# Transposes of linear attention: VectorE blocks of 32 x 32 and transfers through scratch in place of TensorE products

## The chip, the cores and the metric

The kernel runs on one core of a Trainium2 chip. The time is device microseconds (us) of one execution. The kernel before took 2965.23, 2965.16 and 2964.53 us in three runs; the median is 2965.16. The profile is of one further execution.

## The reference

Four residual layers, each with a GroupNorm ahead of it, work on four images of 256 channels and 64 x 64 pixels. The change touches the second layer, and the kernel overlaps it with the first layer of the next image.

```python
x = x + conv_and_nonlocal(gn(x))      # 3x3 convolution, then attention over 4096 x 4096 pixels
x = x + linear_attention(gn(x))       # the layer that is changed
x = x + generated_convolution(gn(x))  # 3x3 depthwise and pointwise, filters made from the image
x = x + mixture_of_experts(gn(x))     # 1x1 convolution

def linear_attention(x):              # x: b, 256, 64, 64
    xn = rmsnorm(x, g_norm)           # over the 256 channels of a pixel
    q, k, v = split(einsum('oc,bchw->bohw', w_qkv, xn))       # 4 heads of 32 each
    q = softmax(q, over the 32 channels of a head)
    k = softmax(k, over the pixels)
    context = einsum('bhdn,bhen->bhde', k, v)
    out = einsum('bhde,bhdn->bhen', context, q * 32 ** -0.5)
    out = einsum('oc,bchw->bohw', w_out, out) + b_out
    return rmsnorm(out, g_out)
```

## The kernel before

**Rounds.** Everything is float32. In round b the generator `attend(b)` (L1068) computes the nonlocal attention of image b in 128 steps: 8 blocks of 512 queries, 16 steps each, a step being 256 keys. A step issues two products of logits (`pf`, L1101), two exponentials on ScalarE (`pr`, L1102), and the products with the values of the step before (`py`). For most blocks these are two wide products (L1217), and VectorE keeps a running sum `tot` of the exponentials (L137); for some blocks of the later images they are eight "turned" products of 129 columns (L1214), which bring the sum with them and need no VectorE. There are 512 steps in the four rounds.

**The chain beside it.** While image b attends, the rest of image b-1 is worked off: `tail(b-1)` is `nonlocal_out`, `linear_attention` (L1352), `generated` and `mixed`, and after it comes the convolution of image b+1. `Chain` (L50) sets these between the steps: each `yield n` of the tail adds n times a rate to a credit, and each whole credit lets one attention step be issued. The rate is 0.775 in rounds 1 and 2 and 1.14 in round 3, where only tail(2) is beside the attention. `yield None` is exactly one step. Tail(3) has no attention beside it (`alone`); its code is another branch. The order of instructions on each engine is the order in which the program issues them (a manual schedule); a wait in one holds back all behind it on its engine. So where a `yield` stands, and what is issued before it, sets what stands beside what. `w.fill` and `w.settle` issue pieces that are held back and play a part in tails 2 and 3 only.

**Linear attention of a chunk of 512 pixels** (8 chunks to an image). `normed` (L1369) applies the GroupNorm, one half of the channels on ScalarE, the other on VectorE, with the channels on the partitions. `turned` (L1379) brings the pixels onto the partitions: eight TensorE transposes, products of 128 x 128 with an identity (L1387), into two PSUM banks; ScalarE squares and sums each pixel's 256 channels (L1389); VectorE clamps, and GpSimd takes the power -1/2 (`rsqrt`, L230 to L232). `tokens` (L1395) multiplies by that root into `xt` on VectorE. `product` and `qk_of` (L1404, L1411) make q and k of the pixels by eight products, exponentials on ScalarE with the root as scale, and the softmax over q on VectorE. `context` (L1427) transposes q with four more products (L1431), which ScalarE copies to `qT` (L1432), and adds k times `xt` to the bank `pctx` in four products of 257 columns, of which the last is a column of ones: the sum of k.

```python
for c in range(NC):
    if c + 1 < NC:
        ahead = normed(c + 1)
...
    yield 0.5
    this = (yield from qk_of(xg, rinv, first)), xt
    first = ()
    if c + 1 < NC:
        xg = ahead
        rinv, banks = turned(xg)
    if last is not None:
        context(c - 1, *last)
```

Four small products then fold the context with the weights of v and of the output into `w2`. In the second loop (L1579) `outputs` (L1509) makes 512 pixels of the output by four products with `w2`, pixels on the partitions, and ScalarE squares them; `root` is as before; `scaled` (L1525) writes `z`, half of it by one VectorE operation, half by two on ScalarE; `added` (L1540) brings the channels back to the partitions by eight transposes (L1545), adds to the image `big` and takes its statistics (`bn_stats`, L1547). The next GroupNorm waits for these: `group_finish` (L396) aggregates them on VectorE and multiplies by a block average on TensorE (`pm`, L413).

**Memory.** `ra` and `rt` are buffers of the convolution and are free during linear attention; the outermost columns of `ra` must be zero when the convolution begins. The pool `k4` has nine buffers of 512 x 4 floats a partition, `k2` four of 512, and PSUM eight banks. `copy_x` (L777) starts DMAs that copy image b+2 into scratch. DMAs are issued by SP (SyncE), one after another, most of them for all parts of the program.

Of the kernel before, what the change touches and what calls it, by code (L numbers as in the profile page):

```python
# [13 lines left out]
P = 128  # L14
NH = 2
# [22 lines left out]
IX1 = HW // MX1  # L38
RW = MX * (IX + 1)
TURNED = 2  # L40
US_A_STEP = 4.35
EASED = 0.68

# [60 lines left out]
def conv_preact_fast(ctx: ExitStack, tc: tile.TileContext, guard, in_range, x, wc, wtpg, ww, wqkv, wout, w1cat, wd2,  # L104
# [153 lines left out]

    rows_d = tc.dram_tile([TY, P, NH, 3, NH * P], F32, name="rows_d")
    filters = tc.dram_tile([TY, P, TX - 2, NH, NH * P], F32, name="filters")  # L260
    taps = wc_s.rearrange("p h (i j) o -> p h i (j o)", i=3)

    NU = TY * NH * 3 * NH * P
# [1088 lines left out]
    def linear_attention(w, b, big, qT, k4, st, sh, sums):  # L1352
# [16 lines left out]
        def normed(c):  # L1369
            cols = bass.ts(c, 512)  # L1370
            xg = k4("xg").rearrange("p (h n) -> p h n", h=NH)
            for h in range(NH):
                if h == 1 and (c == 0 or not alone):
                    nc.vector.tensor_scalar(xg[:, h, :], big[:, h, cols], rstd[:, h:h + 1], nb[:, h:h + 1], ALU.mult, ALU.add)
                else:
                    nc.scalar.activation(xg[:, h, :], big[:, h, cols], AF.Identity, bias=nb[:, h:h + 1], scale=rstd[:, h:h + 1])
            return xg

        def turned(xg):  # L1379

            rinv = sp.tile([P, 4], F32, name="rinv", bufs=4)
            banks = []
            for s in range(2):
                ps = bank("ps_xt").rearrange("p (j c) -> p j c", j=2)
                for j in range(2):
                    for h in range(NH):
                        nc.tensor.transpose(ps[:, j, bass.ts(h, P)], xg[:, h, bass.ts(2 * s + j, P)], ident)  # L1387
                for j in range(2):
                    nc.scalar.activation(junk()[:, 0:NH * P], ps[:, j, :], AF.Square, accum_out=rinv[:, 2 * s + j:2 * s + j + 1])  # L1389
                banks.append(ps)  # L1390
            nc.vector.tensor_scalar(rinv, rinv, 1e-24, None, ALU.max)
            rsqrt(rinv, rinv)
            return rinv, banks

        def tokens(rinv, banks):  # L1395

            xt = k4_wide("xt").rearrange("p (j c) -> p j c", j=4)
            nc.gpsimd.memset(xt[:, :, NH * P:NH * P + 1], 1.0)
            for s in range(2):
# [26 lines left out]

        def context(c, qk, xt):  # L1427

            pt = bank("ps_qt")
            for j in range(4):  # L1430
                nc.tensor.transpose(pt[:, bass.ts(j, P)], qk[:, j, 0:HID], ident)  # L1431
            nc.scalar.copy(qT[:, bass.ts(c, 512)], pt)  # L1432
            for j in range(4):
                nc.tensor.matmul(pctx[:, 0:NH * P + 1], qk[:, j, HID:2 * HID], xt[:, j, :],
                                 start=(c == 0 and j == 0), stop=(c == NC - 1 and j == 3))

        if alone:
            w.fill(1)
            warm(3)
        w.settle()  # L1440
        xg, first = normed(0), ()
        if not alone:
            yield None
        rinv, banks = turned(xg)
        if alone:
            first = [product(xg, j) for j in range(2)]
            next(sums)
        xt = tokens(rinv, banks)
        yield 1
        last = None  # L1450
        for c in range(NC):
            if c + 1 < NC:
                ahead = normed(c + 1)
            if alone:
                next(sums, None)
                if c == 2:
                    checks.append(counted())
                if c in (2, 4, 5):
                    next(checks[0])
            elif b + 2 < B and c % 2 == 0:  # L1460
                copy_x(b + 2, c // 2)
            yield 0.5
            this = (yield from qk_of(xg, rinv, first)), xt
            first = ()
            if c + 1 < NC:
                xg = ahead
                rinv, banks = turned(xg)
            if last is not None:
                context(c - 1, *last)
            if c + 1 < NC:  # L1470
                xt = tokens(rinv, banks)
            last = this
        yield 1
        context(NC - 1, *last)
        w.fill(1)
        rk = sp.tile([P, 1], F32, name="rk", bufs=1)
        nc.vector.reciprocal(rk, pctx[:, NH * P:NH * P + 1])
        cx = k2("cx")[:, 0:NH * P]
        nc.vector.tensor_scalar(cx, pctx[:, 0:NH * P], rk, None, ALU.mult)
        yield None  # L1480
        pt = bank("ps_cx")
        for h in range(NH):
# [17 lines left out]
        if alone:  # L1500
            warm(2)
        w2 = k2("w2")[:, 0:NH * P]
        stt(w2, pw[:, 0:NH * P], HD * float(HD) ** -0.5, bo_s, ALU.mult, ALU.add)
        w.settle()
        yield None

# [18 lines left out]
        def scaled(zr, banks):  # L1525
            z = k4("z").rearrange("p (j o) -> p j o", j=4)
            if alone:
                for j in range(4):
                    src = banks[j // 2][:, j % 2, :]
                    if j < 3:  # L1530
                        nc.scalar.activation(z[:, j, :], src, AF.Copy, scale=zr[:, j:j + 1])
                    else:
                        nc.vector.tensor_scalar(z[:, j, :], src, zr[:, j:j + 1], None, ALU.mult)
                return z
            tt(z[:, 0:2, :], banks[0], zr[:, 0:2].unsqueeze(2).to_broadcast([P, 2, NH * P]), ALU.mult)
            for j in (2, 3):
                nc.scalar.activation(z[:, j, :], banks[1][:, j - 2, :], AF.Copy, scale=zr[:, j:j + 1])
            return z

        def added(c, z, halves=range(NH)):  # L1540
# [34 lines left out]
            w.fill(3)  # L1575
            return st, early, centre

        last = None
        for c in range(NC):  # L1579
            zb = outputs(c)  # L1580
            root(zb[0])
            yield 0.65
            if last is not None:
                added(c - 1, last)
            last = scaled(*zb)
            w.settle()
            if c in (2, 4):
                w.fill(1)
            yield 0.65
        yield 1  # L1590
        added(NC - 1, last)
        return st


# [558 lines left out]
    with tc.manual_schedule(engines={E.PE, E.Activation, E.DVE, E.Pool, E.SP}):  # L2153
        run(Chain(convolve_first).steps())
        run(project(first=True))
        for b in range(B - 1):
            attention = attend(b)
            parts = [tail(b - 1, big, qT), lambda w: convolve(w, b + 1, 0.53)] if b > 0 else [
                scale_weights, filters_across, lambda w: convolve(w, 1, 0.87)]
            if b == 0:  # L2160
                load_x(1)
            run(Chain(both(*parts), 1.365 if b == 0 else 0.775).steps(), attention)
# [594 lines left out]
```

## Time and profile before

The profiled execution took 2965.21 us; the span from its first to its last instruction is 2963.3 us. The granted clock of TensorE was 0.999 over the span.

| what | busy, mean of one | count |
|---|---|---|
| logits products L1101 | 966.4 us, 594 ns | 2048 |
| exponentials L1102 (ScalarE) | 602.8 us, 596 ns | 1024 |
| running sums L137 (VectorE, 1024 columns) | 307.7 us, 1221 ns | 252 |
| transposes of the output L1545 | 29.6 us, 274 ns | 224 records |
| transposes of the queries L1431 | 15.0 us, 273 ns | 100 records |
| copies of the queries L1432 (ScalarE, rounds) | 13.9 us, 580 ns | 24 |
| squares L1389 (ScalarE, 256 columns from PSUM) | 49.2 us, 384 ns, and 195 ns to read the sum | 128 |
| context products L1434, first form | 47.6 us, 380 ns | 200 records |

Each row is a group of instructions of one line and one shape. The duration of a product runs from its start to its modelled end, and products overlap; their spacing is read from the starts in the timeline. A few of TensorE's records are missing from the trace, so the counts of products can be a little low. In the prediction's lines, "idle before, releaser" at the end of a row is the time for which the engine stood still just ahead of the group, and what ended it; in a timeline the first number is the start and the second the length of a run of like instructions.

### The profile page before, as it was taken

How to read it: one execution, taken by the hardware profiler on the slowest of the kernel's cores; microseconds unless marked ns; L12 is line 12 of the kernel's file. 1: busy time of each engine (PE TensorE's matmuls, PEld its weight loads, DVE VectorE, ACT ScalarE, POOL GpSimd, SP SyncE). 2: the span in 40 equal slices, each digit the busy share in tenths (PEclk: the TensorE clock that was granted, in tenths of full speed). 3: DMA queues.
4: the chain of work that ended last, by engine and by line, in shares of the span. 5: the costliest groups of instructions: out<-in, count | busy, mean ns of one | idle time of the engine just before them, and what ended most of it. 6: DMA issues, size and time to landing. Idle time of an engine off the chain costs nothing. (4 is left out here: it accounts for less than half of the span.)

```text
span 2963.3 us, 31330 instructions
## 1 busy us (share of the span) xinstructions
PE 2917.0 (98%) x11638; PEld 1777.7 (60%) x11638; DVE 1786.2 (60%) x2792; ACT 1353.8 (46%) x2720; POOL 189.4 (6%) x235
## 2 busy tenths in 40 slices
PE   7999999999999999999999999999999999999999
PEld 3454555556566666777566666677646544446744
DVE  8737767751545863775355584477344568873585
ACT  2234333345656444225565543333555454433774
POOL 0000000001001000000001000000000100000143
PEclk9999999999999999999999999999999999999999
DMA  6245444324322021111640302211342223225111
GB/s 228 73 88 121 69 62 75 47 32 100 114 40 35 30 79 70 55 57 28 147 93 4 54 12 97 79 50 50 82 107 18 17 28 63 25 32 142 43 67 77
DMA packets 371297, 199.38 MB, mean 67 GB/s; under 512 B 305665, under 2 KB 315649, under 8 KB 367617
## 3 DMA queue, kind: packets, MB, share of 16 engines
q1 hardware_dynamic: 71328, 175.81, 17.5%
q10 hardware_dynamic: 295200, 4.72, 8.0%
q0 software_dynamic: 4608, 16.78, 3.7%
q8 instruction: 93, 1.52, 0.2%
q14 instruction: 68, 0.55, 0.1%
HBM read 131.18 MB, written 82.87 MB: 72 GB/s over the span
## 5 line engine op out<-in xcount | busy, mean ns | idle before, releaser
L1102 ACT ACTIVATE pr<-pf 128x512 f32<-128x512 f32 x1024 | 602.8, 596 | 911.4 <-PE pf L1101 888.7
L1101 PE MATMUL pf<-tpg 128*128 128x512 f32 x2048 | 966.4, 594 | 0.0
L1101 PEld LDWEIGHTS pf<-tpg 128*128 128x128 f32 x2048 | 374.1, 190 | 358.4 <-issue 336.6
L1217 PE MATMUL py<-pr,tpg 128*128 128x512 f32 x1152 | 541.6, 592 | 0.9 <-ACT pr L1102 0.9
L1214 PEld LDWEIGHTS py<-tpg,pr 128*128 128x128 f32 x3584 | 434.9, 192 | 108.0 <-issue 100.7
L1214 PE MATMUL py<-tpg,pr 128*128 128x129 f32 x3584 | 436.3, 275 | 2.4 <-ACT pr L1102 2.4
L1217 PEld LDWEIGHTS py<-pr,tpg 128*128 128x128 f32 x1152 | 218.6, 190 | 277.5 <-issue 268.6
L137 DVE TENSOR_TENSOR tot<-tot,pr 128x1024 f32<-128x1024 f32 x252 | 307.7, 1221 | 98.6 <-ACT pr L1102 98.0
L140 DVE SCALAR_TENSOR_TENSOR dw<-xp,dk,dw 128x1008 f32<-128x1008 f32 x192 | 243.0, 1270 | 7.6 <-ACT dw L1732 3.7
L702 PE MATMUL ps_conv<-v,u 128*128 128x256 f32 x864 | 195.6, 379 | 2.3 <-DVE v L137 2.3
L702 PEld LDWEIGHTS ps_conv<-v,u 128*128 128x128 f32 x864 | 161.5, 190 | 31.3 <-issue 8.4
L232 POOL TENSOR_TENSOR rstd<-rstd,half 128x2 f32<-128x2 f32 x24 | 17.7, 738 | 1953.2 <-DVE rstd L427 1808.7
L1025 PE MATMUL ps_tp<-big,wtpg_s 128*128 128x512 f32 x256 | 116.8, 595 | 4.0 <-ACT big L801 4.0
L137 DVE TENSOR_TENSOR tpg<-ps_g,bg_s 128x512 f32<-128x512 f32 x32 | 22.1, 692 | 155.7 <-PE ps_g L1030 155.7
L1407 PE MATMUL ps_qk<-wqkv_s,xg 128*128 128x256 f32 x496 | 113.7, 379 | 0.0
L140 DVE SCALAR_TENSOR_TENSOR sums<-ps_conv,sums 128x512 f32<-128x512 f32 x72 | 49.8, 691 | 103.9 <-PE ps_conv L702 97.5
L1407 PEld LDWEIGHTS ps_qk<-wqkv_s,xg 128*128 128x128 f32 x496 | 93.7, 190 | 20.3 <-issue 8.4
L1740 PE MATMUL ps_pw<-dw,pk 128*128 128x512 f32 x192 | 86.3, 592 | 0.0
L1025 PEld LDWEIGHTS ps_tp<-big,wtpg_s 128*128 128x128 f32 x256 | 45.9, 190 | 53.4 <-issue 42.1
L1026 ACT ACTIVATE tpg<-ps_tp,btp_s 128x512 f32<-128x512 f32 x64 | 44.0, 687 | 70.9 <-PE ps_tp L1025 70.9
L1167 DVE COPY total<-py 128x2 f32<-128x2 f32 x28 | 4.5, 160 | 115.7 <-PE py L1214 115.7
L1417 ACT ACTIVATE qk<-ps_qk,rinv 128x256 f32<-128x256 f32 x100 | 46.6, 474 | 56.1 <-PE ps_qk L1407 51.9
(467 smaller groups left out, 3348.5 us busy)
## 6 DMA issues: line engine op xcount, KB each, us to landing
u<-filters SPq DMA_DIRECT2D x72, 256.0 KB, 2.7
xp<-in_x_dram SPq DMA_DIRECT2D x16, 1024.0 KB, 8.2
xs_d<-big POOLq DMA_DIRECT2D x32, 512.0 KB, 6.3
wy_d<-wt SPq DMA_DIRECT2D x32, 512.0 KB, 2.8
wy<-wy_d SPq DMA_DIRECT2D x32, 512.0 KB, 4.7
out_dram<-res SPq DMA_DIRECT2D x64, 256.0 KB, 2.0
xs_d<-in_x_dram SPq DMA_DIRECT2D x24, 512.0 KB, 6.7
xs<-xs_d SPq DMA_DIRECT2D x24, 512.0 KB, 5.1
```

Source lines behind the costliest of these rows:

```text
L137: nc.vector.tensor_tensor(o, a, b, op)
L140: nc.vector.scalar_tensor_tensor(o, a, s, b, op0, op1)
L702: nc.tensor.matmul(ps[:, bass.ts(oh, IY * IX)], u[i][:, h, bass.ts(oh, P)], v[:, i, bass.ts(h, IY * IX)], start=(h == 0), stop=(h == NH - 1))
L1025: nc.tensor.matmul(ps, wtpg_s[:, h, k, :], big[:, h, cols], start=(h == 0), stop=(h == NH - 1))
L1026: nc.scalar.activation(tpg[:, k, cols], ps, AF.Identity, bias=btp_s[:, k:k + 1])
L1101: nc.tensor.matmul(pf, phi[:, bass.ts(2 * m + s, P)], theta[:, bass.ts(q, 512)], start=True, stop=True)
L1102: nc.scalar.activation(pr[:, bass.ts(s, 512)], pf, AF.Exp)
L1214: nc.tensor.matmul(py[t // 2][:, t % 2, :], probs[i][:, s * 512 + t * P:s * 512 + (t + 1) * P], g[:, 2 * m + s, :], start=(begin and t % 2 ...
L1217: nc.tensor.matmul(py, g[:, 2 * m + s, 0:P], probs[i][:, bass.ts(s, 512)], start=begin, stop=end)
L1407: nc.tensor.matmul(ps[:, 0:2 * HID], xg[:, h, bass.ts(j, P)], wqkv_s[:, h, 0:2 * HID], start=(h == 0), stop=(h == NH - 1))
L1417: nc.scalar.activation(qk[:, j, :], ps[:, 0:2 * HID], AF.Exp, scale=rinv[:, j:j + 1])
L1740: nc.tensor.matmul(ps, pk[:, h * NH * P + oh * P:h * NH * P + (oh + 1) * P], dw[h][:, bass.ts(s, 512)], start=(h == 0), stop=(h == NH - 1))
```

## The change

In the rounds (tails 0 to 2; tail(3) keeps its branch) the three transposes leave TensorE. Each is made of two parts. VectorE turns the blocks of 32 x 32 of a tile (`nc.vector.transpose`) and writes each of them to its column place in a staging tile. Four DMAs, one for each 32 partitions, store the staging tile in a scratch tensor so that the blocks come to their rows, and one DMA fetches it back (`turned_d` for the image, `q_d` for the queries, `z_d` for the output).

- Image: `corners` (two VectorE transposes of 512 columns), `sent` (4 x 130 KB), `fetched` (520 KB). The staging tile is a quarter of `ra` and `rt`, `quarters[3]`; what is fetched goes to the other three in turn. A column of ones lies in each of four groups, so the context products have TW = 260 columns. `lengths` squares from SBUF in place of PSUM; `unit` multiplies by the root in place, four VectorE operations of 256 columns for two of 512.
- Queries: `q_corners`, `q_sent`, `q_fetched` straight into `qT`; the ScalarE copy goes.
- Output: `z_corners` (one transpose of 1024 columns), `z_sent` (4 x 128 KB), `z_fetched`, `z_added`, which reads SBUF. The columns of `w2` are permuted for it, in two operations for one. `scaled` is now three operations on ScalarE and one on VectorE.
- Loops: the image is normalised and turned two chunks ahead of its use, its transfer fetched one ahead; the output is added two chunks behind its products. The yields change: two of 0.5 and one of 1 before the first chunk (before: one step and 1), 0.7 twice a chunk in the output loop (0.65), and 0.5 and 1.2 at its end (1). The rate of rounds 1 and 2 is 0.785 (0.775). At the end GpSimd zeroes the outer columns of `ra` again.

```diff
+        def corners(xg):
+            s = quarters[3]
+            for h in range(NH):
+                nc.vector.transpose(s.rearrange("p (c j o) -> p c j o", c=4, j=4)[:, :, :, bass.ts(h, 32)],
+                                    xg[:, h, :].rearrange("p (j c e) -> p c j e", j=4, c=4))
+            return s
+
+        def sent(c, s):
+            for a in range(4):
+                nc.sync.dma_start(out=turned_d[c, :, :, a, :].rearrange("c e n -> e c n"),
+                                  in_=s[bass.ts(a, 32), :].rearrange("p (c n) -> p c n", c=4))
+
+        def fetched(c):
+            x = quarters[c % 3]
+            nc.sync.dma_start(out=x, in_=turned_d[c].rearrange("c e a n -> (c e) (a n)"))
+            return x.rearrange("p (a j o) -> p a j o", a=4, j=4)
+
+        def lengths(x):
+            rinv = sp.tile([P, 4], F32, name="rinv", bufs=4)
+            for j in range(4):
+                nc.scalar.activation(junk()[:, 0:NH * P].rearrange("p (a o) -> p a o", a=4), x[:, :, j, 0:NH * 32],
+                                     AF.Square, accum_out=rinv[:, j:j + 1])
...
+        def unit(x, rinv):
+            for j in range(4):
+                nc.vector.tensor_scalar(x[:, :, j, 0:NH * 32], x[:, :, j, 0:NH * 32], rinv[:, j:j + 1], None, ALU.mult)
...
+            xgs = {0: normed(0)}
+            s = corners(xgs[0])
             yield 0.5
+            sent(0, s)
+            xgs[1] = normed(1)
+            s = corners(xgs[1])
+            yield 0.5
+            xs = {0: fetched(0)}
+            sent(1, s)
+            yield 1
+            rinv = lengths(xs[0])
+            last, turn = None, None
+            for c in range(NC):
+                if c + 1 < NC:
+                    xs[c + 1] = fetched(c + 1)
+                if c + 2 < NC:
+                    xgs[c + 2] = normed(c + 2)
+                    s = corners(xgs[c + 2])
+                unit(xs[c], rinv)
+                if b + 2 < B and c % 2 == 0:
+                    copy_x(b + 2, c // 2)
+                yield 0.5
+                if turn is not None:
+                    q_sent(c - 1, turn)
+                if c + 2 < NC:
+                    sent(c + 2, s)
+                qk = yield from qk_of(xgs.pop(c), rinv)
+                turn = q_corners(qk)
+                if c > 0:
+                    q_fetched(c - 1)
+                if last is not None:
+                    context(c - 1, *last)
+                if c + 1 < NC:
+                    rinv = lengths(xs[c + 1])
+                last = qk, xs.pop(c)
+            q_sent(NC - 1, turn)
+            yield 1
+            q_fetched(NC - 1)
+            context(NC - 1, *last)
...
-        last = None
+        s, zts = None, {}
         for c in range(NC):
             zb = outputs(c)
             root(zb[0])
-            yield 0.65
-            if last is not None:
-                added(c - 1, last)
-            last = scaled(*zb)
+            if c > 0:
+                z_sent(c - 1, s)
+            yield 0.7
+            if c > 0:
+                zts[c - 1] = z_fetched(c - 1)
+            if c > 1:
+                z_added(c - 2, zts.pop(c - 2))
+            s = z_corners(scaled(*zb))
             w.settle()
             if c in (2, 4):
                 w.fill(1)
-            yield 0.65
-        yield 1
-        added(NC - 1, last)
+            yield 0.7
+        z_sent(NC - 1, s)
+        yield 0.5
+        zts[NC - 1] = z_fetched(NC - 1)
+        z_added(NC - 2, zts.pop(NC - 2))
+        yield 1.2
+        z_added(NC - 1, zts.pop(NC - 1))
```

More of the change, by code (lines that the diff above doesn't have):

```diff
@@ L40 @@
 TURNED = 2
+TW = 4 * (NH * 32 + 1)
 US_A_STEP = 4.35
@@ L260, in conv_preact_fast @@
     filters = tc.dram_tile([TY, P, TX - 2, NH, NH * P], F32, name="filters")
+    turned_d = tc.dram_tile([NQ, 4, 32, 4, 4 * (NH * 32 + 1)], F32, name="turned_d")
+    q_d = tc.dram_tile([NQ, 4, 32, 4, P], F32, name="q_d")
+    z_d = tc.dram_tile([NQ, 4, 32, 4, NH * P], F32, name="z_d")
     taps = wc_s.rearrange("p h (i j) o -> p h i (j o)", i=3)
@@ L1377, in normed, with q_corners, q_sent, q_fetched @@
             return xg
+        quarters = [t.rearrange("p h y x -> p (h y x)")[:, bass.ds(i * 4 * TW, 4 * TW)] for t in (ra, rt) for i in range(2)]
+        def corners(xg):
[17 more added lines that the diff above has]
+                                     AF.Square, accum_out=rinv[:, j:j + 1])
+            nc.vector.tensor_scalar(rinv, rinv, 1e-24, None, ALU.max)
+            rsqrt(rinv, rinv)
+            return rinv
+        def unit(x, rinv):
+            for j in range(4):
+                nc.vector.tensor_scalar(x[:, :, j, 0:NH * 32], x[:, :, j, 0:NH * 32], rinv[:, j:j + 1], None, ALU.mult)
+        def q_corners(qk):
+            s = k2("q_turn")
+            nc.vector.transpose(s.rearrange("p (a j e) -> p a j e", a=4, j=4),
+                                qk[:, :, 0:HID].rearrange("p j (a r) -> p a j r", a=4))
+            return s
+        def q_sent(c, s):
+            for k in range(4):
+                nc.sync.dma_start(out=q_d[c, :, :, k, :].rearrange("a r n -> r a n"),
+                                  in_=s[bass.ts(k, 32), :].rearrange("p (a n) -> p a n", a=4))
+        def q_fetched(c):
+            nc.sync.dma_start(out=qT[:, bass.ts(c, 512)], in_=q_d[c].rearrange("a r c n -> (a r) (c n)"))
         def turned(xg):
@@ L1427, in context @@
         def context(c, qk, xt):
-            pt = bank("ps_qt")
+            if alone:
+                pt = bank("ps_qt")
+                for j in range(4):
+                    nc.tensor.transpose(pt[:, bass.ts(j, P)], qk[:, j, 0:HID], ident)
+                nc.scalar.copy(qT[:, bass.ts(c, 512)], pt)
             for j in range(4):
[L1431 to L1434, printed above, removed]
+                nc.tensor.matmul(pctx[:, 0:NH * P + 1 if alone else TW], qk[:, j, HID:2 * HID], xt[:, j, :] if alone else xt[:, :, j, :],
                                  start=(c == 0 and j == 0), stop=(c == NC - 1 and j == 3))
@@ L1439, in linear_attention @@
             warm(3)
[L1440 to L1445, printed above, removed]
+            w.settle()
+            xg, first = normed(0), ()
+            rinv, banks = turned(xg)
             first = [product(xg, j) for j in range(2)]
             next(sums)
-        xt = tokens(rinv, banks)
-        yield 1
-        last = None
[L1451 to L1454, printed above, removed]
+            xt = tokens(rinv, banks)
+            yield 1
+            last = None
+            for c in range(NC):
+                if c + 1 < NC:
+                    ahead = normed(c + 1)
                 next(sums, None)
@@ L1459, in linear_attention @@
                     next(checks[0])
-            elif b + 2 < B and c % 2 == 0:
-                copy_x(b + 2, c // 2)
-            yield 0.5
[L1463 to L1467, printed above, removed]
-            if last is not None:
[L1469 to L1473, printed above, removed]
@@ L1474, in linear_attention @@
-        context(NC - 1, *last)
+                yield 0.5
+                this = (yield from qk_of(xg, rinv, first)), xt
+                first = ()
+                if c + 1 < NC:
+                    xg = ahead
+                    rinv, banks = turned(xg)
+                if last is not None:
+                    context(c - 1, *last)
+                if c + 1 < NC:
+                    xt = tokens(rinv, banks)
+                last = this
+            yield 1
+            context(NC - 1, *last)
+        else:
+            w.settle()
+            nc.gpsimd.memset(quarters[3].rearrange("p (k o) -> p k o", k=16)[:, :, NH * 32:TW // 4], 1.0)
+            xgs = {0: normed(0)}
+            s = corners(xgs[0])
+            yield 0.5
+            sent(0, s)
[4 more added lines that the diff above has]
+            sent(1, s)
+            yield 1
+            rinv = lengths(xs[0])
+            last, turn = None, None
+            for c in range(NC):
+                if c + 1 < NC:
+                    xs[c + 1] = fetched(c + 1)
[14 more added lines that the diff above has]
+                    q_fetched(c - 1)
+                if last is not None:
+                    context(c - 1, *last)
+                if c + 1 < NC:
+                    rinv = lengths(xs[c + 1])
+                last = qk, xs.pop(c)
+            q_sent(NC - 1, turn)
+            yield 1
+            q_fetched(NC - 1)
+            context(NC - 1, *last)
@@ L1475, in linear_attention @@
         w.fill(1)
         rk = sp.tile([P, 1], F32, name="rk", bufs=1)
-        nc.vector.reciprocal(rk, pctx[:, NH * P:NH * P + 1])
         cx = k2("cx")[:, 0:NH * P]
-        nc.vector.tensor_scalar(cx, pctx[:, 0:NH * P], rk, None, ALU.mult)
+        if alone:
+            nc.vector.reciprocal(rk, pctx[:, NH * P:NH * P + 1])
+            nc.vector.tensor_scalar(cx, pctx[:, 0:NH * P], rk, None, ALU.mult)
+        else:
+            nc.vector.reciprocal(rk, pctx[:, NH * 32:NH * 32 + 1])
+            nc.vector.tensor_scalar(cx.rearrange("p (h a r) -> p h a r", h=NH, a=4),
+                                    pctx[:, 0:TW].rearrange("p (a o) -> p a o", a=4)[:, :, 0:NH * 32].rearrange("p a (h r) -> p h a r", h=NH),
+                                    rk, None, ALU.mult)
@@ L1502, in linear_attention @@
         w2 = k2("w2")[:, 0:NH * P]
-        stt(w2, pw[:, 0:NH * P], HD * float(HD) ** -0.5, bo_s, ALU.mult, ALU.add)
+        if alone:
+            stt(w2, pw[:, 0:NH * P], HD * float(HD) ** -0.5, bo_s, ALU.mult, ALU.add)
+        else:
+            for h in range(NH):
+                stt(w2.rearrange("p (a h r) -> p h a r", a=4, h=NH)[:, h], pw[:, bass.ts(h, P)].rearrange("p (a r) -> p a r", a=4),
+                    HD * float(HD) ** -0.5, bo_s[:, bass.ts(h, P)].rearrange("p (a r) -> p a r", a=4), ALU.mult, ALU.add)
         w.settle()
@@ L1534, in scaled @@
                 return z
-            tt(z[:, 0:2, :], banks[0], zr[:, 0:2].unsqueeze(2).to_broadcast([P, 2, NH * P]), ALU.mult)
-            for j in (2, 3):
-                nc.scalar.activation(z[:, j, :], banks[1][:, j - 2, :], AF.Copy, scale=zr[:, j:j + 1])
+            for j in range(4):
+                src = banks[j // 2][:, j % 2, :]
+                if j == 1:
+                    nc.vector.tensor_scalar(z[:, j, :], src, zr[:, j:j + 1], None, ALU.mult)
+                else:
+                    nc.scalar.activation(z[:, j, :], src, AF.Copy, scale=zr[:, j:j + 1])
             return z
@@ L1576, in linear_attention, with z_corners, z_sent, z_fetched @@
             return st, early, centre
-        last = None
+        def z_corners(z):
+            s = quarters[3][:, 0:CH]
+            nc.vector.transpose(s.rearrange("p (k j e) -> p k j e", k=8, j=4), z.rearrange("p j (k r) -> p k j r", r=32))
+            return s
+        def z_sent(c, s):
+            for k in range(4):
+                nc.sync.dma_start(out=z_d[c, :, :, k, :].rearrange("a r n -> r a n"),
+                                  in_=s[bass.ts(k, 32), :].rearrange("p (a n) -> p a n", a=4))
+        def z_fetched(c):
+            x = quarters[c % 3][:, 0:CH]
+            nc.sync.dma_start(out=x, in_=z_d[c].rearrange("a r c n -> (a r) (c n)"))
+            return x.rearrange("p (c h t) -> p h c t", c=4, h=NH)
+        def z_added(c, zt):
+            cols = bass.ts(c, 512)
+            for h in range(NH):
+                mine = big[:, h, cols]
+                stt(mine.rearrange("p (c t) -> p c t", c=4), zt[:, h], gains[:, 1, h:h + 1],
+                    mine.rearrange("p (c t) -> p c t", c=4), ALU.mult, ALU.add)
+                nc.vector.bn_stats(st[:, h, c, :], mine)
+        s, zts = None, {}
         for c in range(NC):
@@ L1581, in linear_attention @@
             root(zb[0])
-            yield 0.65
-            if last is not None:
-                added(c - 1, last)
-            last = scaled(*zb)
+            if c > 0:
[6 more added lines that the diff above has]
+            s = z_corners(scaled(*zb))
             w.settle()
@@ L1588, in linear_attention @@
                 w.fill(1)
-            yield 0.65
-        yield 1
-        added(NC - 1, last)
+            yield 0.7
+        z_sent(NC - 1, s)
+        yield 0.5
+        zts[NC - 1] = z_fetched(NC - 1)
+        z_added(NC - 2, zts.pop(NC - 2))
+        yield 1.2
+        z_added(NC - 1, zts.pop(NC - 1))
+        if b + 2 < B:
+            nc.gpsimd.memset(ra[:, :, :, 0:1], 0.0)
+            nc.gpsimd.memset(ra[:, :, :, HW + 1:HW + 2], 0.0)
         return st
@@ L2161, in conv_preact_fast @@
                 load_x(1)
-            run(Chain(both(*parts), 1.365 if b == 0 else 0.775).steps(), attention)
+            run(Chain(both(*parts), 1.365 if b == 0 else 0.785).steps(), attention)
             while next(attention, False):
```

## Prediction

> **What bounds the kernel now.** I read the page's first block, then TensorE's waits, then the timeline inside the two loops that the change rewrites (L1451 and L1579).
>
> ```profile
> PE 2917.0 (98%) x11638; PEld 1777.7 (60%) x11638; DVE 1786.2 (60%) x2792; ACT 1353.8 (46%) x2720; POOL 189.4 (6%) x235
> ```
>
> The waits of PE add up to some 40 us, 16.9 of them once at the start; none lies in the tails of images 0 to 2. So in the rounds TensorE sets the time, and its order of work is fixed when the program is built: a product that leaves makes all behind it earlier, and one that waits makes all behind it late. The next lines are one chunk of the output loop in tail(0).
>
> ```profile
> 902.16 1.04 PE L1545 MATMUL ps_zt<-ident,z 128*128 128x128 f32 x8
> ...
> 903.04 1.89 PE L1515 MATMUL ps_o<-w,xp 128*128 128x256 f32 x8
> ...
> 904.11 0.39 ACT L1517 ACTIVATE junk<-ps_o 128x256 f32<-128x256 f32 x1 [0.81 <-PE ps_o L1515]
> ...
> 904.77 1.88 PE L1101 MATMUL pf<-tpg 128*128 128x512 f32 x4
> ...
> 906.00 1.28 ACT L1102 ACTIVATE pr<-pf 128x512 f32<-128x512 f32 x2
> ...
> 906.47 1.85 POOL L232 TENSOR_TENSOR zr<-zr,half 128x4 f32<-128x4 f32 x1 [4.05 <-DVE zr L1522]
> 906.48 1.88 PE L1217 MATMUL py<-pr,tpg 128*128 128x512 f32 x4
> ...
> 908.20 1.04 PE L1545 MATMUL ps_zt<-ident,z 128*128 128x128 f32 x8
> ...
> 908.36 0.84 ACT L1537 ACTIVATE z<-ps_o,zr 128x256 f32<-128x256 f32 x2 [1.07 <-POOL zr L232]
> ```
>
> See the starts, not the durations: eight transposes take 902.16 to 903.04, the four output products (eight records) to 904.77, the attention step (two logits, two values) to 908.20. So 0.88 + 1.73 + 3.43 = 6.04 us, with no gap. ScalarE squares for 2.0 us, does the step's two exponentials while GpSimd takes the root, and then scales.
>
> **What leaves TensorE.** Per image of the rounds, eight chunks lose 8 transposes of the image, 4 of the queries and 8 of the output: 20 x 8 x 3 = 480. A row says 273 ns each:
>
> ```profile
> L1387 PE MATMUL ps_xt<-ident,xg 128*128 128x128 f32 x248 | 32.6, 273 | 0.6 <-ACT xg L1376 0.6
> ...
> L1422 DVE TENSOR_REDUCE qs<-qk 128x16 f32<-128x512 f32 x25 | 17.1, 685 | 61.4 <-ACT qk L1417 61.4
> ...
> L1374 DVE TENSOR_SCALAR xg<-big,rstd,nb 128x512 f32<-128x512 f32 x24 | 12.9, 539 | 0.1
> ```
>
> That is one transpose from end to end; they overlap, and the starts give 0.88 / 8 = 0.11 us. [...] By it the sum is 480 x 0.275 = 132 us, by the spacing **480 x 0.11 = 52.8 us**; what a removal gives back is the spacing. The wider context products (260 columns for 257) cost 1.2% of 24 x 1.73, 0.5 us.
>
> **What VectorE gets.** No transpose on VectorE is in this trace. [...] Context chunk: before 3.74 (0.54 + 2 x 0.69 + 0.17 + 0.69 + 0.25 + 0.69). After: minus 1.38, plus three transposes of 512 (2.07), plus four scalings of 256 at 0.41 (line through 539 at 512 and 804 at 1024): 6.1. Against TensorE's 3.43 + 1.73 + 0.75 steps x 3.43 = 7.7, and 1.22 more where a step has a running sum: close, but under. Output chunk: 0.17 + 0.48 + 1.22 + 4 x 0.69 = 4.6, plus 1.22. On ScalarE the copies of the queries go (0.58 a chunk), the squares from SBUF cost about 0.12 more each (719 against 596 at 512 columns), a third of the scalings comes (0.42).
>
> **What the transfers cost.** [...] But the strides stay with VectorE; these transfers move runs of 512 to 1040 bytes, so the rows here decide: 256 KB stored lands in 2.0, 512 KB in 2.8, 512 KB loaded in 4.7 with another load beside it, 256 KB in 2.7. A send is four issues of 0.33 and the last one's landing, 3.1; a fetch about 4.2. Ends for one relay: 5.5 (2.8 + 2.7) and 12. In steady running both lie a chunk ahead. SP issues 10 transfers a chunk, 3.3 us, behind one another: a send waits for VectorE, and the attention's sums and stores wait behind it; nobody needs those for a step. The copies of image b+2 (6.7 to landing) go ahead of the sends and may make VectorE wait one to two us, inside its slack.
>
> **Where the wait goes.** Four places, counted from the orders of instructions.
>
> 1. Start of the context loop. Before: root, image normalised, transposes, without a gap. Now, from the end of the pv product: 1.3 to nb, 0.8 normalised on ScalarE, 1.4 transposes, 3.1 send, 4.2 fetch, 2.5 squares (4 x 0.63), then on ScalarE 0.8 normalising and 1.2 exponentials (the root beside them), 0.5 first exponential of qk: 15.9. TensorE has two steps and one chunk of qk, 10.3, and is then out of banks: 1 py, 1 context, 2 logits whose exponentials stand behind the squares on ScalarE, 4 qk. Stall 5.6 in tails 0 and 1; tail(2) has three steps, 2.2.
> 2. Inside it VectorE and ScalarE run at 7 to 7.5 of 7.7: 0.9, 0.9, 1.5.
> 3. Output loop. In the new order the step's exponentials mostly stand after the scaling, not before it, so nothing covers the root: squares 2.0, root 2.3 (906.10 to 908.36 above), three scalings 1.26, exponentials 1.2: 6.7 a chunk, where TensorE needs 1.73 + 3.43 = 5.2. Six such chunks, less one step of lead (3.4): 5.7 stalled, of the 7.0 that the transposes save here. tail(2) has twelve steps for eight chunks, half of them covering: 2.0.
> 4. End of the output loop. From the last scaling: 1.3 VectorE, 3.1, 4.3 back, 2.8 added, 0.9 aggregated, 0.3: 12.7 before the pm product can run; TensorE has 6.3 of steps left. Stall 6.4; tail(2) has two steps more, 1.3.
>
> Sum: 18.6 + 18.6 + 7.0 = **44.2 given back of 52.8**. Pacing (0.785, more steps per output chunk) costs nothing: the convolution behind is paced by its own VectorE work and its last products stand at the same attention step, 120 of 128, in both orders. Removed work on PSUM banks only helps.
>
> **Sum.** The profiled execution took 2965.2, its span 2963.3. 2963.3 - 52.8 + 0.5 + 44.2 = 2955.2, and 1.9 around it: **2957**. The median of the runs shown, 2965.16, is the same as the profiled one. 0.2% is 5.9 us (what a measurement can tell from no change): 2959.3 is the border.
>
> **Rivals.**
> - *The relays are hidden* (10%): shorter relays (5.5 us) and an even spread of exponentials. All 52.8 would be 2913; half the stalls kept, 2935. For it: VectorE is busy 60%, DMA 2 to 3 tenths in these slices. Against: items 1 and 4 are chains without other work in them.
> - *VectorE becomes the bound* (27%): a 4-byte transpose takes two cycles per element. Then a context chunk costs 1.6 more, 7.7 plus sums, past TensorE's 7.7; about 9 a tail there, 2 in the output loop, 2.5 at both ends: 13.5 x 3 = 40, so 2997. From 0.8 us for 512 columns on (8.6 / 24 chunks / 3) it is slower than before. For it: no row shows the operation. [...]
> - *Relays longer than priced* (18%): 1 KB runs, copies ahead of them, lanes waited for. Each us of relay costs 2 in each of two tails and about 1 in the third, 5 in all; at 10.5 instead of 7.3 it is +16: 2973.
> - My forecast, stalls of 35 to 55, 45%: 2947 to 2968, its likeliest value 2957.
>
> That the change doesn't do what it says has no room: the order has 480 fewer products.
>
> Chances: faster takes most of the forecast (0.34) and the hidden relays (0.10); same is the rest of the forecast's middle and a little of the third rival, 0.14; slower 0.42. Range 2925 (half hidden) to 2997 (the second rival's value).
>
> **What would show it.** L1387, L1431 and L1545 left only with image 3; VectorE transposes near 0.69 and 1.22 us (a value above 0.8 for 512 is the second rival); waits of PE, absent before, three times before the first qk exponentials (5 to 6 us, 2 in the third) and before pm L413 by VectorE's aggregation (6); value products L1217 waiting for pr in the output loops, about one to two us a chunk; landing times of the sends near 2 and fetches near 4. PE's busy sum should fall by about 53 us whatever happens. I am wrong if the pm wait is missing, or if attention steps in the context loop wait for VectorE throughout.

## The result

The changed kernel takes 2997.59 us in the median of four runs (2996.76 to 2998.74), against 2964.93 for the kernel before in the same sessions: a ratio of 1.011, interval 1.0093 to 1.0128. It is slower by 32.7 us, where 8 less had been forecast. The profiled execution has a span of 2995.0 us, 31.7 more than before.

First some lines of the changed kernel's profile: busy time of each engine, then some groups (line, engine, operation, tiles, count, busy time and mean in ns, idle time ahead of the group and what ended it), then DMA issues with KB of each and the median time to landing in us.

```profile
PE 2885.3 (96%) x11158; PEld 1734.3 (58%) x11158; DVE 1849.4 (62%) x2939; ACT 1341.5 (45%) x2720; POOL 189.8 (6%) x218
```

```profile
L1388 DVE STREAM_TRANSPOSE rt<-xg 128x512 f32<-128x512 f32 x48 | 34.1, 710 | 51.5 <-DMA turned_d<-rt 46.7 <-ACT pr L1106 2.3 <-ACT xg L1380 1.1
L1681 DVE STREAM_TRANSPOSE rt<-z 128x1024 f32<-128x1024 f32 x24 | 29.9, 1245 | 5.9 <-ACT junk L1615 2.6 <-ACT z L1638 1.5 <-DMA z_d<-rt 0.4
```

```profile
turned_d<-rt SPq DMA_DIRECT2D x96, 130.0 KB, 2.7
...
z_d<-rt SPq DMA_DIRECT2D x96, 128.0 KB, 2.4
ra<-turned_d SPq DMA_DIRECT2D x18, 520.0 KB, 3.6
...
ra<-z_d SPq DMA_DIRECT2D x18, 512.0 KB, 3.4
...
inv<-sum_d ACTq DMA_DIRECT2D x18, 256.0 KB, 12.1
```

VectorE's transposes cost what the sum took (0.71 and 1.25 us for 0.69 and 1.22). A send takes 4.2 us (image) or 3.8 (output) in the median from its first issue to its last landing, where the sum took 3.1 (an issue of a store costs SyncE near 0.46 us, not 0.33), and a fetch 3.6 or 3.4, where it took 4.2: together near the sum's 7.3. TensorE's busy time fell by 31.7 us, not by 53; of the difference, 14.8 us are products that ran at half the clock (last column of the table), and the rest was not traced. The waits of TensorE are the new thing (us in all, times, the longest):

```profile
PE pm L413 <- DVE mv L138: 26.5, 2, 13.6
PE ps_ctx L1485 <- DVE qk L138: 18.7, 3, 9.1
PE pm L413 <- DVE mv L351: 16.6, 1, 16.6
PE ps_qk L1457 <- ACT pr L1106: 7.4, 4, 3.0
```

The third line is the wait at the start, which was there before. The first is two waits, one at the end of the output loop in each of tails 0 and 1; of the second, 8.5 and 9.1 us are one wait in each of the same tails, in the sixth of the eight chunks of the context loop. Tail 2 has neither. A round, taken from the first projection product of one round to that of the next, tells the same:

| round | before | after | difference | idle of TensorE added | products at half clock |
|---|---|---|---|---|---|
| 1 (tail 0) | 711.3 | 732.9 | +21.6 | 31.4 | 4.6 |
| 2 (tail 1) | 711.4 | 733.3 | +21.9 | 29.0 | 8.5 |
| 3 (tail 2) | 611.8 | 600.2 | -11.6 | 3.6 | 1.7 |

(Round 3 is taken to the end of its attention. The last column is worked out in windows of 1 us: busy time times one less the granted clock.) So the change gains where it stands beside the long last round, and loses twice as much in each of the two others. Round by round the sum is 160 x 0.11 = 17.6 us taken from TensorE, 0.2 for the wider products, and these two columns; 3.0, 1.8 and 0.5 us of the three rounds stay unexplained.

**The wait in the context loop.** The timeline of all engines in tail 0 (start, length of the run, engine, line, tiles, count, idle before and its releaser):

```profile
837.81 14.20 SPq L1423 DMA_DIRECT2D q_d<-q_turn  x4
...
851.87 1.03 PE L1457 MATMUL ps_qk<-wqkv_s,xg 128*128 128x256 f32 x4
...
852.11 1.86 SPq L1394 DMA_DIRECT2D turned_d<-rt  x4
...
856.15 1.46 DVE L1388 STREAM_TRANSPOSE rt<-xg 128x512 f32<-128x512 f32 x2 [11.84 <-DMA turned_d<-rt]
...
860.69 0.69 DVE L138 TENSOR_TENSOR qk<-qk,qs 128x512 f32<-128x512 f32 x1
...
861.43 3.84 PE L1485 MATMUL ps_ctx<-rt,qk 128*128 128x260 f32 x8 [8.54 <-DVE qk L138]
```

Four small stores of the queries take SyncE from 837.81 to 852.01. The waits of SyncE in this stretch say why:

```profile
SPq L1423 <- DMA inv<-sum_d: 12.1, 1, 12.1
```

`inv<-sum_d` (L1138) is the read-back of the softmax sums of the block of queries that has just ended. ScalarE's queue issued it at 835.13 and it lands after 15.6 us. It has nothing to do with the queries: no tile is shared. What they share is a completion counter, the semaphore that tells of a transfer's landing. The trace names it for every DMA: those of SyncE and ScalarE take eight of them in turn (100, 101, 103, 104, 105, 107, 108 and 109, 101 or 102 transfers each), in the order of the program. The read has number 104, the first of the four stores 103, the second again 104. The first landed at 844.63, with the read still under way; the second was issued at 850.72, and the read had landed at 850.70. So the counter stopped the queue, and not the DMA engines. The same is seen in tail 1 (counter 103, 1584.16 and 1584.17). Behind it in SyncE's queue stands the store of the next image chunk; VectorE, which needs that chunk's staging tile, stands still for 11.84 us; the queries' softmax stands behind VectorE's transposes; the context product waits for that. The read was in the kernel before too, as its list of DMA issues shows:

```profile
inv<-sum_d ACTq DMA_DIRECT2D x18, 256.0 KB, 11.4
```

There SyncE never waited for it.

**The wait before pm.** The same view at the end of the output loop of tail 0:

```profile
941.89 0.37 ACTq L1138 DMA_DIRECT2D inv<-sum_d  x1
...
943.75 2.06 SPq L1686 DMA_DIRECT2D z_d<-rt  x4
...
950.87 0.34 SPq L1691 DMA_DIRECT2D ra<-z_d  x1
...
956.72 0.75 DVE L141 SCALAR_TENSOR_TENSOR big<-ra,gains,big 128x512 f32<-128x512 f32 x1 [8.70 <-DMA ra<-z_d]
...
960.33 0.58 PE L413 MATMUL pm<-mv,avg 128*128 128x2 f32 x2 [13.55 <-DVE mv L138]
```

The next block's read starts 1.9 us ahead of the last stores. Here none of the relay's transfers waits for the read's counter, but each takes longer: the last store is issued by 945.8 and the fetch can go only at 950.87, 5 us later, where 2.4 is the median; the fetch takes 5.8 for 3.4. That is 13 us from the first store to the landing, then 3.6 of adding and statistics, and TensorE has run out of other work at 946.8. That the read crowds these transfers on the DMA engines is inferred from their times.

### The profile page after: what moved, and what is told of

The parts are those of the page before. It is cut to its first block, busy times and chain, and to the rows that moved or that the text cites. A ratio compares the mean times of both kernels' runs of the same rounds, so it can differ in the third digit from the quotient of the medians.

```text
span 2995.0 us, 31153 instructions
## 1 busy us (share of the span) xinstructions
PE 2885.3 (96%) x11158; PEld 1734.3 (58%) x11158; DVE 1849.4 (62%) x2939; ACT 1341.5 (45%) x2720; POOL 189.8 (6%) x218
## 5 line engine op out<-in xcount | busy, mean ns | idle before, releaser
L1034 PEld LDWEIGHTS ps_g<-wtpg_s,big 128*128 128x128 f32 x512 | 62.2, 192 | 15.3 <-issue 15.3
```

Source lines behind the costliest of these rows:

```text
L1034: nc.tensor.matmul(ps[:, j, :], big[:, h, bass.ts(4 * c + j, P)], wtpg_s[:, h, 2, :], start=(h == 0), stop=(h == NH - 1))
```

## Experiments

**The read taken away.** Two ways to do it: let the sums come back in one plain piece, or let no block of images 1 and 2 need them (TURNED is the number of blocks that do).

```diff
-            nc.scalar.dma_start(out=inv.rearrange("r (p k) -> r p k", k=4), in_=sum_d[at].rearrange("p (r k) -> r p k", k=4))
+            if b in (1, 2):
+                nc.scalar.dma_start(out=inv, in_=sum_d[at])
...
```

> In images 1 and 2 the sums of the softmax come back as they lie, in one plain read of 256 KB, instead of turned in pieces of 16 bytes (so the denominators of two blocks of queries an image are wrong). Theory A (the 15 us of this read hold up SyncE's queue in the context loop and the last relay of the output): the wait of the context product for qk falls from 8.5 and 9.1 us to under 1.5, the wait before pm from 13.6 and 12.9 to 7 to 9, the clock stays above 0.9 in the first place; 2 x (7.5 + 2.3 clock + 5 + 1) = 32 less, 2966. Theory B (the relay is long by itself, or VectorE is late): both waits stay within 2 us of what they are, 2992 to 2998.

```diff
-TURNED = 2
+TURNED = 0
```

> All query blocks of images 1 and 2 take the turned value products, so that no sums are made on VectorE, written, or read back in those rounds. Theory A: the same as the plain read, about 2966, plus 2 x 32 steps x 0.07 us of longer steps (4.5) less what VectorE's 60 sums of 1.22 us held up (up to 5): 2963 to 2970. Theory B: if VectorE is what is late, this run is at least 10 us faster than the plain read; if it is the relay alone, both waits stay and it is 2997 to 3003.

Measured: 2969.35 us (2965.35 to 2974.50, 20 runs; ratio 1.0018, 1.0011 to 1.0024) with the plain read, 2967.92 (2965.10 to 2972.72, 20 runs; 1.0011, 1.0005 to 1.0018) with all blocks turned. The first is 3.4 us above theory A's 2966 and far from theory B's 2992; the second lies in A's range. With the plain read SyncE goes through the same place like this:

```profile
837.36 2.46 SPq L1426 DMA_DIRECT2D q_d<-q_turn  x4
839.92 5.16 SPq L1397 DMA_DIRECT2D turned_d<-rt  x4
```

and TensorE waits like this:

```profile
PE pm L413 <- DVE mv L138: 18.1, 2, 9.2
...
PE ps_ctx L1488 <- DVE qk L138: 2.8, 4, 1.0
```

The long wait for qk is gone (1.0 at most), though the four stores of the queries land late here too (6.2 to 7.6 us after their issue). What they no longer do is wait for the counter, which the plain read gives back after 3.3 us. The waits before pm are 9.2 and 9.0, a little above what was expected. So this one transfer of the attention costs 28 us of the changed kernel's 32.7. The run with all blocks turned is 1.4 us faster, within the spread of the runs, and its waits before pm are 6.5 and 5.1. So the running sums, their stores and their reads together hold the relay's end up by some 3 to 4 us more; they were not tried apart.

**The read moved.** The same read, in its own form, four steps later, with later pauses cut.

```diff
             nc.sync.dma_start(out=sum_d[at], in_=inv)
-            yield
+            later = 4 if b in (1, 2) else 0
+            for _ in range(1 + later):
+                yield
...
```

> The changed kernel with one thing moved: in rounds 1 and 2 the turned read of the sums is issued four attention steps later, behind the last chunk of the context loop in the first block and behind the output's last transfers in the second; four steps of later waiting are cut for it, so the block's product comes where it came. Nothing is left out. Theory A (it is this read's place beside the transfers): as with the plain read, the wait of 8.5 and 9.1 us in the context loop falls under 2, the one before pm to 8 to 10, 2969 (2966 to 2974). Rival (the read's 15 us cost the same wherever they lie, through the attention's own chain): 2985 or more.

Measured: 2972.27 us (2969.21 to 2973.73, 10 runs; 1.0024, 1.0014 to 1.0033). The four moved reads are still long: they land after 11.3 to 13.0 us, where they took 15.2 to 15.9. The context loop's wait falls to 1.0 and the waits before pm to 9.3 and 8.9. It is where the read stands that costs. In the output loop new waits of 2.3 and 1.6 us for z appear, about the 2.9 us by which this run is above the plain read.

**The output undone, in two paces.** The old output loop on TensorE (L1545 of before, with its `scaled`, its yields of 0.65 and the unpermuted `w2`); image and queries stay changed. The pixels of a chunk keep the order in which the queries came back, so the output is added at other pixels than it should be.

> The output's transposes are put back on TensorE with the old loop; image and queries stay by VectorE and transfers. Theory A: 192 transposes come back (21.1 us), the waits before pm (13.6 + 12.9) go and with them the half clock behind them (2 x 2.6) and the 3.6 us that the output loops wait for z; the context loop's waits stay unless the block's end moves: 2997.6 + 21.1 - 35.3 = 2983. Theory B (the prediction's size for this part, stalls 14 to 15 in all): 3000 to 3006.

Measured: 2998.42 us (2996.70 to 2998.64; 1.0114, 1.0097 to 1.0130): no gain at all, far from theory A's 2983 and just under theory B's 3000. The waits before pm were gone, but others had come at the end of the rounds, 4.8 us in each, with 6.8 us of half clock behind them. The order of instructions explains it: the old yields are shorter, and with the rate left at 0.785 the chain's later pieces fell on other steps. The convolution's last group mean stood at step 127 of 128, where it stands at 125 both before and after. One number put it back:

```diff
-            run(Chain(both(*parts), 1.365 if b == 0 else 0.785).steps(), attention)
+            run(Chain(both(*parts), 1.365 if b == 0 else 0.775).steps(), attention)
```

> As the run with the output's transposes on TensorE, with the rate of rounds 1 and 2 at 0.775 as in the kernel before. By the order of instructions, 0.785 with the shorter yields had moved the convolution's last group mean from step 125 of the round's 128 to 127, and 0.775 moves it back. Theory A: the waits at the round's end that the run at 0.785 showed (4.8 us, and a low clock behind them) go; what is left is the context loop's waits and clock, 18 us a round, against 10.6 of transposes gone: 2965 + 2 x 7.5 - 6.7 = 2973. Rival (the image's and queries' part costs this much by itself): 2990 or more.

Measured: 2989.60 us (2987.60 to 2990.52; 1.0084, 1.0067 to 1.0100). The end of the rounds is as before, so the pacing was worth 8.8 us, but the value is 17 above theory A's and at the rival's 2990. The waits name the missing part:

```profile
PE ps_ctx L1485 <- DVE qk L138: 16.8, 4, 7.8
PE ps_qk L1457 <- ACT qk L1467: 16.7, 6, 4.6
```

At 0.775 the first chunk comes a step earlier, and the relay's lead at the start is shorter: the waits for the first qk grow from 2.7 and 3.0 us to 3.7 and 4.6, and two more of 3.2 and 4.1 come in the loop. SyncE again waits for the read of the sums, this time with a copy of the image after next:

```profile
SPq L784 <- DMA inv<-sum_d: 10.9, 1, 10.9
```

That copy and the read have no data in common either; they have the same counter (101). So the image's and queries' part alone costs 24.4 us net (2989.6 less the 2965.2 of the kernel before in that session), and the output's part adds 8.0.

**The waits filled.** Idle products (a matrix of ones by the identity, 128 columns) are put into the two long waits of tails 0 and 1, to keep TensorE's clock up. They write where nothing is read. The edit shows those of the first wait.

```diff
+                if c == 6 and b < 2:
+                    for i in range(65):
+                        nc.tensor.matmul(pctx[:, 3 * P:4 * P], ones, ident, start=False, stop=False)
                 if last is not None:
                     context(c - 1, *last)
```

> Idle products of 128 columns fill the two long waits of tails 0 and 1: 65 ahead of the sixth chunk's context products, 100 ahead of pm, about 7 and 11 us, less than the waits. Nothing else changes, so whatever the waits wait for comes at the same time. Theory A (an idle TensorE runs at half clock for some 5 us after its work is back): the granted clock stays near 1 and 2 x (2.3 + 2.6) = 10 us go: 2988. Rival (the lower clock costs nothing, as the products behind are not the bound): 2996 to 2999.

Measured: 3018.77 us (3017.36 to 3024.54). The fill was mis-sized: 65 such products took 14.7 us, twice their spacing as transposes, so they ran on after the wait. With 33 and 50:

> The fill of the last run was twice as long as meant: 65 idle products took 14.7 us from start to end, 0.226 each. Here 33 and 50 of them, 7.5 and 11.3 us, under the waits of 8.5 to 9.1 and 12.9 to 13.6. Theory A (half clock after an idle TensorE costs 2.3 to 2.6 us a time): the clock stays at 0.99 or more over the span, PE's rest of the waits is 1 to 2 us each, 2988 (2986 to 2990). Rival (the clock costs nothing): 2996 to 2999.

Measured: 2993.92 us (2992.45 to 2995.29; 1.0096, 1.0079 to 1.0112), 3.7 below the changed kernel's 2997.59, between both values. The runs of the two kernels do not overlap, but their intervals do, so the size of the gain is uncertain. The half clock itself is in the trace. The windows of the changed kernel around the first of these waits (stretch; busy time of PE, PEld, DVE, ACT, POOL; granted clock; DMA share and GB/s):

```profile
852.00:854.00 2.00, 0.89 (x5) 0.44 (x3) 0.00 (x0) 0.00 (x0) 0.00 (x0) 1.00 0.71 164
854.00:856.00 2.00, 0.00 (x0) 0.00 (x0) 0.00 (x0) 0.00 (x0) 0.00 (x0) 0.95 0.91 235
856.00:858.00 2.00, 0.00 (x0) 0.00 (x0) 1.81 (x4) 0.00 (x0) 0.00 (x0) 0.50 0.65 204
...
864.00:866.00 2.00, 2.00 (x6) 1.53 (x6) 1.70 (x4) 1.90 (x5) 0.00 (x0) 0.50 0.91 319
866.00:868.00 2.00, 2.00 (x11) 1.77 (x10) 1.83 (x4) 1.70 (x7) 0.00 (x0) 0.99 0.68 184
```

TensorE stops at 852.9, the clock halves at 855.8, the work is back at 861.4, and full speed at 866.0: 2.9 us of standing still, then 4.6 of work. Before pm it is 4.6 and 4.7. In the three tails the granted clock is 0.50 six times: for 10.2 us from 855.8 and from 1589.7, for 13.7 from 951.4 and from 1685.2, for 6.8 from 1535.0 and for 3.4 from 2289.4. How much standing still brings it these traces do not settle: in tail 2 a wait of 2.2 us stands ahead of it, while one of 2.7 in tail 0 has full clock behind it. What the filling gave back was less than the 10 us expected of it. By the windows of 1 us the changed kernel loses 14.8 us to the half clock in the three tails, and the filled one still 9.8: the waits of 2 to 3 us that it keeps, as one of 2.88 us behind which the two logits take 3.1 us in place of 1.7, have the half clock (0.50) behind them too.

**Versions put together.** All blocks turned, and in tails 0 and 1 the last output chunk by eight TensorE transposes (its pixels in the queries' order, as above), so that no relay stands ahead of pm; rate 0.79:

> All query blocks turned in images 1 and 2 (no sums to read back), and in tails 0 and 1 the last of the eight output chunks goes by TensorE's transposes, so that no relay stands at the end of the loop; rate 0.79, at which the last group mean stands at step 125 again. Theory A: against the run with all blocks turned (2968), the waits of 6.5 and 5.1 before pm and their clock (2 x 2) go, 2 x 0.9 us of transposes come back, one step less stands at the loop's end: 2956 (2952 to 2959). Rival (the wait before pm is VectorE's adding and statistics, not the relay): 2964 to 2968.

Measured: 2955.56 us (2951.91 to 2958.94, 6 runs; 0.9970, 0.9957 to 0.9982). As expected: the waits before pm are 0.5 at most, and the last chunk's transposes wait 1.4 and 2.5 for z. Only tail 2 changed, with the rate of rounds 1 and 2 at 0.775 again:

```diff
-            st = yield from linear_attention(w, b, big, qT, k4, st, sh, sums)
+            st = yield from (linear_attention if b == 2 else linear_attention_before)(w, b, big, qT, k4, st, sh, sums)
```

> Only image 2's tail, which has the attention of round 3 beside it, uses the changed layer; tails 0 and 1 keep the old one and the rate 0.775. Theory A: rounds 1 and 2 as in the kernel before, round 3 shorter by the 11.6 us that the changed kernel showed: 2953 (2952 to 2955). Rival (the gain of round 3 hangs on what rounds 1 and 2 leave behind): 2960 or more.

Measured: 2951.88 us (2950.73 to 2953.29; 0.9955, 0.9938 to 0.9971). Rounds 1 and 2 are the old 711.3 and 711.4, round 3 is 599.3. The gain of round 3 stands alone. Last, in tails 0 and 1 only the pieces that need no short relay (the image back on TensorE, the last chunk of queries and output too), and tail 2 as changed:

> A version put together from what the runs showed: in tails 0 and 1 the image is transposed by TensorE as before, the queries (seven chunks of eight) and the output (seven of eight) by VectorE and transfers, the last chunk of both by TensorE, so that nothing waits for a relay at the start or at the end; tail 2 as changed; query blocks as before; rate 0.79, at which the last group mean stands at step 125. Theory A: rounds 1 and 2 each lose 84 transposes, 9.2 us, against some 2 us of waits in the output loop and 1 to 2 in the convolution; round 3 loses 12: 2965 - 2 x 6 - 12 = 2941 (2936 to 2946). Rival (a send in the output loop still holds TensorE up through SyncE's queue when the sums are read back): 2950 or more.

Measured: 2948.91 us (2947.43 to 2952.32; 0.9946, 0.9930 to 0.9963). It beats both kernels, and is 8 above what was expected, just below the rival's 2950. SyncE still waits 4.0 us for the read in each context loop, but TensorE no longer waits there, and the clock stays full in tails 0 and 1. Yet each of rounds 1 and 2 gains 1.3 to 1.8 us instead of 6: TensorE stands still for 10.2 and 10.5 us in them, 4.0 in the kernel before, against 9.2 us of transposes gone:

```profile
PE ps_zt L1765 <- DVE z L1674: 4.2, 2, 2.1
...
PE ps_conv L706 <- DVE v L138: 3.8, 2, 1.9
PE ps_conv L706 <- issue: 2.7, 2, 1.4
```

The last chunk's transposes wait 2.1 us for z and pm 1.0, and the convolution, which at this rate has 32 steps in place of 34, waits 3.3 in place of 1.2. Its interval overlaps that of the version with only tail 2 changed; the two were not timed together.

## Why the prediction was wrong

The range ended at 2997.0, the value of the rival in which VectorE becomes the bound; the two cycles an element from which it is worked out no run shows. That the time fell beside it is chance: 0.71 us for 512 columns is below the 0.8 at which that rival began to decide. That a transpose on VectorE costs 0.69 us (512 columns) and 1.22 (1024) was the author's estimate, the times of the sum over q (L1422, 685 ns) and of the running sum (L137, 1221 ns) in the kernel before; the runs showed 0.71 and 1.25. Nor does a run show the 0.275 us a transpose behind the sum of 132 us; in the kernel before it is 273 ns from start to end, and 0.11 us from start to start, from which the 52.8 us are worked out. Of the forecast's sum, what leaves TensorE holds: where round 3 can use it, 17.6 less the waits and the half clock shown gives the measured 11.6 within 1 us. What failed is the part given back, place by place (tails 0 / 1 / 2, us):

| place | predicted | measured |
|---|---|---|
| 1. start of the context loop | 5.6 / 5.6 / 2.2 | 2.7 / 3.0 / 2.2 |
| 2. inside it | 0.9 / 0.9 / 1.5 | 11.4 / 9.7 / 0 |
| 3. output loop | 5.7 / 5.7 / 2.0 | 1.8 / 1.4 / 1.4 |
| 4. before pm | 6.4 / 6.4 / 1.3 | 13.6 / 12.9 / 0 |
| convolution behind | 0 | 2.0 / 2.0 / 0 |
| half clock | 0 | 4.6 / 8.5 / 1.7 |

- The step that failed first is the sentence that in steady running sends and fetches "lie a chunk ahead" and that the attention's sums wait behind them. Of what the new transfers themselves wait behind, the prediction named only the copies of image b+2 (one to two us), and not the turned read of the sums with its 11.4 us, which stopped SyncE's queue for 12 us through the counter. It put the inside of the context loop at 0.9 us, and 11.4 and 9.7 were measured. Taking the long read away brought 28 us, moving it 25. Places 2 and 4 in tails 0 and 1 are where the first and the second block of queries end; that was in the order of instructions and could have been counted.
- Place 4 was named rightly, and its wait was to be 6.4 us. With the plain read it is 9.0 to 9.2. Of the chain of 12.7 us, the store and the fetch were taken at 3.1 and 4.3: with the plain read they take 4.8 (934.79 to 939.55) and 3.8. With the running sums and their transfers gone too, in the run with all blocks turned, the waits are 6.5 and 5.1, the size of the forecast. Tail 2, with two steps more, needs no wait.
- Place 3 was too large by its root: 2.3 us was taken from one chunk of the kernel before and set for all. In tail 0 ScalarE waits 1.3 us for GpSimd's root in four of the eight chunks and 2.1 to 2.7 in the other four. So fewer chunks are slow than was taken; the 1.8 us measured were not worked out from this.
- Place 1 was put at about twice what was measured in tails 0 and 1; the third tail is met to 0.1. TensorE waits there for the exponentials, as the forecast said; which of its terms was too long was not worked out.
- That the pacing "costs nothing" was wrong by 2 us a round in the convolution. How sharp the pacing is, the two runs with the output undone show: 8.8 us for one hundredth of the rate.
- The half clock was left out of the sum, and the sentence that the busy sum falls by about 53 us "whatever happens" fell with it (31.7). It takes 14.8 us in the three tails; filling the two long waits brought 3.7.
- The rival of longer relays (2973) is nearest in mechanism; it spoke of "copies ahead of them, lanes waited for", but priced them as a little more on each relay, not as one read that stops the queue for 12 us.

In the context loop the trace shows the counter as what stops SyncE's queue, in three kernels and with two different transfers behind the read; no run changed the counter alone. Before pm the counter plays no part, and what lengthens the transfers there was not tried apart.

## What to carry to other kernels

Before a transfer is put into a loop in which the bounding engine waits for its result, list every transfer that can be under way at that place, with its time to landing and its completion counter, and look for the longest: here one held a queue until it had landed (12.1 and 12.5 us), though no data was shared. A relay through scratch was cheap here where whole steps of other work lay behind it and dear at the start and the end of a loop; putting the last chunk on the old path took the wait at the end away. When yields change, count where the last pieces of the chain fall before judging the edit itself.

## What was not expected of the hardware

A read of 256 KB in pieces of 16 bytes took 15.6 us to land. Before pm in tail 0 the stores beside it took 5.0 to 5.6 us (2.2 to 3.3 beside the plain read) and the fetch 5.8 (3.8). From 846 to 848 us, with no other data transfer under way, the DMA engines moved 27 GB/s for it. A transfer issued by SyncE stood still for up to 12.5 us because one issued by ScalarE held the same completion counter. An idle product of 128 columns took 0.226 us from start to start, where a transpose of the same shape takes 0.11. Behind a wait of TensorE of 2.2 us in tail 2 (to 2288.3) the granted clock was 0.50 for 3.4 us (from 2289.4).
